# Layer 0's attention in two parts a batch with a written TensorE order, and its experts in groups of one and three batches

## The chip, the cores and the metric

The kernel runs on one core of one Trainium2 chip. The metric is device time in microseconds, from the first to the last instruction of an execution. The times of the kernel before are 1352.45 us (median of three runs, 1351.14 to 1359.07). A profiled execution is a run by itself and has its own time.

## What is computed

Four layers follow each other on x (4 batches of 512 tokens, 128 wide). Each layer adds a cross-attention with a context of 154 rows and then a mixture of eight experts; both read a layer norm of x without weights:

```python
x = x + _L0_xattn_ref(_layernorm(x), ctx_1024, ...)
x = x + _L0_ffn_ref(_layernorm(x), ...)
...
```

Layer 0's attention scores every token against the context rows, takes the softmax over the context and, with the maxima of the scores, one softmax over the tokens of a batch:

```python
A = jax.nn.softmax(Sim, axis=2)
hq_hat = jnp.einsum('bij,bjd->bid', A, decoder_hq)
Batt = jax.nn.softmax(jnp.max(Sim, axis=2), axis=1)
hc_bar = jnp.einsum('bi,bid->bd', Batt, encoder_hc)[:, None, :]
feats = jnp.concatenate([encoder_hc, hq_hat, encoder_hc * hq_hat, encoder_hc * hc_hat], axis=-1)
hcq = feats @ W_qv + b_qv
```

Layer 0's experts are gated (silu of one product times another, then a down projection), with the best two of eight for every token. Layers 1 to 3 have 16 heads of attention; layer 1 takes one expert a token with a capacity, layers 2 and 3 take two.

## The kernel before, in words

All data are float32. A tile is 128 tokens, so a batch has four tiles and the whole x has sixteen; x stays in SBUF, one buffer a batch.

The experts run on blocks of 128 tokens of one expert. route() finds for a group of batches (a "half": batches 0 and 1, or 2 and 3) the best experts, gives each token a slot in an array of blocks (at most 2 x 8 + 7 = 23 blocks a half in layer 0) and queues one row transfer for each tile and choice: an indirect DMA on POOL that scatters 128 rows of xn to buf in DRAM (line 722). experts() loads four blocks of tokens at a time (line 840, which waits for all scatters of the half), transposes them, and for every block loads the weights of its expert by a register (516 KB, line 869, three buffers), multiplies up (line 877), applies the activation (lines 900 and 905), multiplies down (line 916), copies the result (line 925) and stores it to ybuf (line 928). gather() queues indirect DMAs that bring the rows back (line 953), and combine() adds them to x with their weights (line 971).

Row transfers wait in the list rows_due. row_transfers(n, behind) starts the next n of them, and makes each wait for the instruction behind, so that they are spread over other work. They go behind copies: of attention (lines 1034, 1039, 1072, 1080), of a block's result (line 924) or of a narrow tile (line 375). A call without behind starts what is left.

Generators carry the interleaving. route() and experts() stop at each yield, and the class Steps advances them. In the main loop (from line 1356) the two halves of a layer follow each other: attention of all batches with the routing of half 0 beside it; experts of half 0, with the routing of half 1 advanced two steps for every two blocks; experts of half 1, with the gathers and sums of half 0 beside them; then the next layer's attention of batch 0, with the gathers and sums of half 1 beside it.

Layer 0's attention (layer0_setup, lines 974 to 1085) has prepare(), which gives a batch's normed x, its transpose and the scores, and tile_of(): scaled softmax, transposes (1033, 1038), the product with the context (1041, 1042), the maximum over the batch by a transpose and a broadcast matmul (1048 to 1052), the second softmax (1057), its sum over tokens (1060, 1061), the weights wc (1070), twelve matmuls with W_qv (1078) and the residual (1081, 1083). attend_first() (line 1278) calls these with nothing written about the order of engines: the framework's scheduler places the instructions on every engine. From layer 1 on attend_all() fixes the order of TensorE and ScalarE (layers 2 and 3 also that of VectorE) by the order in which the code is called.

In layer 1's attention (narrow_period, line 435) a tile's scores, maxima (294), exponentials (308), transposes (371) and products with the values (408) are laced with those of the tile before. The parts of the next batch (masks; norm and values; xnT; keys and queries) are handed out over the four tiles of a batch (line 1193).

Of the kernel before, what the change touches and what calls it, by code (L numbers as in the profile page):

```python
# [9 lines left out]
F32 = mybir.dt.float32  # L10
# [9 lines left out]
P = 128  # L20
# [9 lines left out]
NH = NT // 2  # L30
EPS = 1e-5
NEG = -1e20
BLK = (2 * NH + E - 1, NH + E - 1)
UPS = (2, 1, 1, 1)
NF = (4, 4, 2, 4)
PER = (1, 2, 2, 2)


# [9 lines left out]
def tile_xattn_moe_stack(ctx: ExitStack, tc: tile.TileContext, a: dict, out: bass.AP):  # L48
# [101 lines left out]
    for base, sign in ((0, 1), (D // H - 1, -1)):  # L150
# [17 lines left out]
    fill = const.tile([P, E, NH], F32, name="fill")  # L168
    nc.gpsimd.iota(
        fill, pattern=[[0, E], [P, NH]], base=0, channel_multiplier=0, allow_small_or_imprecise_dtypes=True  # L170
# [6 lines left out]
    nth = const.tile([1, BLK[0], E], F32, name="nth")  # L177
    nc.gpsimd.iota(
        nth, pattern=[[1, BLK[0]], [0, E]], base=0, channel_multiplier=0, allow_small_or_imprecise_dtypes=True
# [59 lines left out]
    def norm(src, found, pool=None):  # L239
        mv, rstd = found  # L240
        xn = (pool or xnp).tile([P, NI, D], F32, tag="xn", name="xn", bufs=3 if pool else 2)
        for i in range(NI):
            nc.vector.tensor_scalar(
                xn[:, i, :], src[:, i, :], mv[:, i, 0:1], rstd[:, i : i + 1], ALU.subtract, ALU.mult
            )
        return xn
# [23 lines left out]
    class Tile:  # L270
# [31 lines left out]
        def exp(self, g):  # L302
            if g == 0:
                self.pr = p2.tile([P, H, S2], F32, tag="probs", name="probs")
            for s in range(min(3, 8 - 3 * g)):
                for j in range(2):
                    h = self.at.heads(None, 3 * g + s, j)
                    nc.scalar.activation(  # L308
# [5 lines left out]
                    )  # L314

# [44 lines left out]
        def take_ends(self, engine):  # L360
            self.tails = p2.tile([self.rows, 4, P], F32, tag="tails", name="tails")
# [174 lines left out]
    def attention64(b, gather_x, wq, wk, wv, wo, add):  # L536
# [36 lines left out]
        def values_ends():  # L573
# [3 lines left out]
            for r in range(2):  # L577
                rows = slice(64 * r, 64 * r + 64)
                nc.tensor.matmul(q[rows, :], ct2[:, b], wv[:, r * 512 : (r + 1) * 512], start=True, stop=True)
# [6 lines left out]
            at.vt = at.vt.rearrange("p c s d -> p (c s d)")  # L586

# [35 lines left out]
    def rsm(name, *shape, dt=F32):  # L623
        return rt.tile([P, *shape], dt, tag=name, name=name)

    def top(lg):

        m = rt.tile([P, NH], F32, tag="m", name="m", bufs=4)
        nc.vector.tensor_reduce(m, lg, AX.X, ALU.max)
        eq = rt.tile([P, NH, E], F32, tag="eq", name="eq", bufs=4)  # L630
        nc.vector.tensor_tensor(eq, lg, bc(m, 2, E), ALU.is_equal)
        nc.vector.tensor_tensor(eq, eq, bc(rev_e, 1, NH), ALU.mult)
        r = rt.tile([P, NH], F32, tag="r", name="r", bufs=4)
        nc.vector.tensor_reduce(r, eq, AX.X, ALU.max)
        oh = rt.tile([P, NH, E], F32, tag="oh", name="oh", bufs=4)
# [5 lines left out]
    def row_transfers(n=2 * NH, behind=None):  # L641
# [9 lines left out]
    def route(layer, half, wg, bg, b2):  # L651

        lg = rsm("lg", NH, E)
        found = [stats(x[2 * half + k]) for k in range(B // 2)]
        yield
        xns = [norm(x[2 * half + k], found[k], rt) for k in range(B // 2)]
        yield  # L660
        xnTs = [transposed(xn) for xn in xns]
        yield
        for k, xnT in enumerate(xnTs):
            q = ps_tr()
            for i in range(NI):
                nc.tensor.matmul(q[:, i * E : (i + 1) * E], xnT[:, i * P : (i + 1) * P], wg, start=True, stop=True)
            o = lg[:, k * NI : (k + 1) * NI, :]
            qv = q[:, 0 : NI * E].rearrange("p (i e) -> p i e", i=NI)
            if bg is None:
                nc.vector.tensor_copy(o, qv)  # L670
            else:
                nc.vector.tensor_tensor(o, qv, bc(bg, 1, NI), ALU.add)
        yield
# [3 lines left out]
        sel = rsm("sel", NH + 1, E, dt=BF16)  # L677
        nc.vector.memset(sel[:, NH, :], 0.0)
        if layer == 1:
            nc.vector.tensor_copy(sel[:, 0:NH, :], oh1)  # L680
        else:
            yield
            lg2 = rsm("lg2", NH, E)
# [3 lines left out]
            nc.vector.tensor_tensor(sel[:, 0:NH, :], oh1, oh2, ALU.add)  # L687
# [3 lines left out]
        n = (NH + 1) * E  # L691
        q = ps_tr()
        nc.tensor.matmul(q[:, 0:n], before, sf, start=True, stop=False)
        for s in range(1, NH + 1):
            nc.tensor.matmul(q[:, s * E : n], ones_b, sf[:, 0 : n - s * E], start=False, stop=(s == NH))
        rk = rsm("rk", NH + 1, E)
# [736 lines left out]
```

## Time and profile before

| what | value |
|---|---|
| median of three runs | 1352.45 us |
| the profiled execution | 1282.47 us |
| its span | 1280.8 us |
| its mean granted TensorE clock | 0.917 |
| busy: TensorE, weight loads, VectorE, ScalarE, GpSimd | 1089.4, 896.9, 731.6, 565.3, 253.6 us |
| moved by DMA | 126.77 MB, mean 99 GB/s |

The profiled execution is 70 us shorter than the median of the runs. Stage by stage, from the chain of waits: layer 0's attention until about 106 us, its experts until about 259, layer 1's attention until about 479, its experts until about 560; layer 2 until about 891 and layer 3 to the end. In the profile's lines a start time and a duration in us come first; PE is TensorE, PEld its weight loads, DVE VectorE, ACT ScalarE, POOL GpSimd, SPq the queue of SyncE on which plain DMAs are issued. In a timeline the bracket at a line's end is the idle time before the instruction and what ended it. An x count of matmuls counts passes; a float32 matmul takes two where its form isn't a transpose.

### The profile page before, as it was taken

The page shows a single profiled execution, that of the slowest core. Times are in us where ns is not written, and L with a number is a line of the kernel's source. Part 1 is how long each engine was busy: PE and PEld are TensorE (multiplying, and loading weights), DVE is VectorE, ACT ScalarE, POOL GpSimd, SP SyncE. Part 2 cuts the span into 40 slices and gives each one's busy share as a digit, 9 for nine tenths or more (in the row PEclk, how much of TensorE's full clock was granted, in tenths as well). Part 3 has the DMA queues.
Part 4 walks back from the last instruction along what each step waited for, and adds up shares of the span by engine and source line. Part 5 has one row for each costly group of instructions (what it writes and reads, how often), then busy time and mean ns, then how long its engine had stood idle before and what let it go on. Part 6 is the DMA issues. An engine that isn't in the chain of part 4 may idle for free.

```text
span 1280.8 us, 26318 instructions
## 1 busy us (share of the span) xinstructions
PE 1089.4 (85%) x9351; PEld 896.9 (70%) x9351; DVE 731.6 (57%) x2012; ACT 565.3 (44%) x2264; POOL 253.6 (20%) x281
## 2 busy tenths in 40 slices
PE   4787998977878888889999998966899999899990
PEld 3657998933435448787878777855778788789890
DVE  6554646567666763335665776424476576646352
ACT  2113433454554543546656565321656665532230
POOL 2041315023000010232000004045220000402334
PEclk8767999988898988998999999887999999999996
DMA  7023786721100314433112214444421111334762
GB/s 228 1 81 113 216 253 189 207 94 25 23 19 26 100 38 119 133 110 84 35 35 55 64 37 123 123 150 133 127 55 45 41 35 35 109 95 143 209 191 60
DMA packets 136064, 126.77 MB, mean 99 GB/s; under 512 B 12538, under 2 KB 115583, under 8 KB 135551
## 3 DMA queue, kind: packets, MB, share of 16 engines
q1 hardware_dynamic: 128767, 110.39, 30.5%
q0 software_dynamic: 7168, 14.69, 3.9%
q8 instruction: 77, 1.26, 0.4%
q14 instruction: 52, 0.43, 0.1%
HBM read 101.31 MB, written 23.72 MB: 98 GB/s over the span
## 4 chain that ended last, share of the span: by engine, by line
PE 59%; DVE 12%; DMA 9%; issue 8%; ACT 5%; POOL 5%; SPq 2%; POOLq 0%; DVEq 0%
PE sc L877 11%; PE av L916 6%; PE tr L371 6%; PE sc L607 5%; PE av L408 5%; PE tr L425 5%; PE sc L592 3%; DMA yg<-ybuf,su 3%; POOL yg L953 3%; ACT probs L308 3%; DVE nm L294 3%; PE sc L1175 2%; DMA w<-in_up 2%; PE av L390 2%; PE tr L358 2%
## 5 line engine op out<-in xcount | busy, mean ns | idle before, releaser
L308 ACT ACTIVATE probs<-sc,nm 128x154 f32<-128x154 f32 x768 | 286.9, 403 | 162.7 <-DVE nm L294 162.5
L877 PE MATMUL sc<-tokT,w 128*128 128x128 f32 x1528 | 201.3, 286 | 8.7 <-DMA w<-in_up 3.6
L877 PEld LDWEIGHTS sc<-tokT,w 128*128 128x128 f32 x1528 | 189.0, 200 | 15.5 <-ACT eg L900 5.2
L294 DVE TENSOR_REDUCE nm<-sc 128x6 f32<-128x924 f32 x144 | 142.6, 1007 | 74.8 <-PE sc L607 49.1
L308 ACT ACTIVATION_READ_ACCUMULATOR probs<-sc,nm 128x1 f32 x768 | 168.3, 219 | 0.0
L916 PE MATMUL av<-w,hT 128*128 x1160 | 155.3, 279 | 3.2 <-DVE hT L905 2.5
L953 POOL DMA_INDIRECT yg<-ybuf,su x112 | 106.7, 952 | 246.5 <-ACT pT L267 59.9
L722 POOL DMA_INDIRECT buf<-xn,su x112 | 109.6, 979 | 227.0 <-DVE eb L745 97.3
L916 PEld LDWEIGHTS av<-w,hT 128*128 128x128 f32 x1160 | 141.9, 193 | 8.9 <-issue 4.7
L236 POOL TENSOR_TENSOR rstd<-ve,nhalf 128x4 f32<-128x4 f32 x32 | 33.0, 1032 | 547.3 <-DVE ve L234 429.6
L264 DVE COPY pT<-tr 128x512 f32<-128x512 f32 x160 | 106.9, 684 | 45.3 <-PE tr L371 41.5
L408 PE MATMUL av<-pT,vm 128*64 128x128 f32 (+1 forms) x1536 | 106.2, 284 | 22.5 <-DVE pT L264 22.4
L371 PE MATMUL tr<-ident,probs 128*128 128x128 f32 x768 | 123.1, 291 | 1.5 <-DVE rT L337 1.5
L371 PEld LDWEIGHTS tr<-ident,probs 128*128 128x128 f32 x768 | 86.1, 146 | 33.4 <-issue 21.7
L408 PEld LDWEIGHTS av<-pT,vm 128*64 128x64 f32 (+1 forms) x1536 | 63.8, 126 | 55.7 <-DVE pT L264 30.9
L900 ACT ACTIVATE eg<-sc,w 128x128 f32<-128x128 f32 x184 | 52.9, 368 | 89.5 <-PE sc L877 82.1
L607 PE MATMUL sc<-kT,qT 64*128 64x154 f32 x1024 | 87.1, 308 | 4.8 <-ACT probs L308 4.8
L905 DVE SCALAR_TENSOR_TENSOR hT<-sc,w,eg 128x128 f32<-128x128 f32 x184 | 56.2, 342 | 51.0 <-ACT eg L900 51.0
L607 PEld LDWEIGHTS sc<-kT,qT 64*128 64x128 f32 x1024 | 71.3, 189 | 15.8 <-issue 9.9
L592 PE MATMUL sc<-xnT,wq 128*128 128x128 f32 x512 | 73.6, 303 | 4.7 <-ACT probs L308 2.3
L592 PEld LDWEIGHTS sc<-xnT,wq 128*128 128x128 f32 x512 | 67.3, 212 | 10.2 <-issue 3.6
L425 PE MATMUL tr<-wo,aT 128*128 128x128 f32 x512 | 66.2, 284 | 1.6 <-DVE xnT L256 1.3
(255 smaller groups left out, 1432.2 us busy)
## 6 DMA issues: line engine op xcount, KB each, us to landing
w<-in_up SPq DMA_DIRECT2D x46, 516.0 KB
w<-in_up SPq DMA_DIRECT2D x76, 258.0 KB
rep<-rd SPq DMA_DIRECT2D x64, 256.0 KB
tok<-buf SPq DMA_DIRECT2D x36, 256.0 KB
ybuf<-ys SPq DMA_DIRECT2D x58, 128.0 KB
w<-in_down SPq DMA_DIRECT2D x3, 2048.0 KB
w<-in_up SPq DMA_DIRECT2D x46, 128.0 KB
ybuf<-ys SPq DMA_DIRECT2D x52, 64.0 KB
```

Of the source, the lines that this page charges most:

```text
L264: return nc.vector.tensor_copy(o, i)
L294: nc.vector.tensor_reduce(self.at.heads(self.nm, g, n), self.sc[g][:, :, 0 : n * S2].rearrange("p j (s k) -> p j s k", s=n), AX.X, ALU.max ...
L308: nc.scalar.activation(self.pr[:, h, :], self.sc[g][:, j, s * S2 : (s + 1) * S2], AF.Exp, bias=self.nm[:, h : h + 1], accum_out=self.rs[:, ...
L371: nc.tensor.transpose(q[:, t * P : (t + 1) * P], self.pr[:, h, 0:P], ident)
L408: nc.tensor.matmul(av[rows, cols], v, self.pT[n][:, t, :], start=False, stop=last)
L425: nc.tensor.matmul(o[:, 0:D], self.aT[:, c, :], self.at.wo[:, c, :], start=(c == 0), stop=(c == self.nb - 1))
L592: nc.tensor.matmul(sc[:, c // 4, c % 4 * P : (c % 4 + 1) * P], wq[:, c * P : (c + 1) * P], at.xnT[:, i * P : (i + 1) * P], start=True, sto ...
L607: nc.tensor.matmul(sc[:, j, s * S2 : (s + 1) * S2], at.qT[i][rows, c, :], at.kT[rows, c, :], start=True, stop=True)
L722: ins = nc.gpsimd.indirect_dma_start(out=buf[half], out_offset=bass.IndirectOffsetOnAxis(ap=su[:, t : t + 1], axis=0), in_=xns[t // NI][:, ...
L877: nc.tensor.matmul(dst, w[:, b, at : at + P], xT, start=True, stop=True)
L916: nc.tensor.matmul(y[:, b * D : (b + 1) * D], hT[:, fc, :], w2[:, bass.ds(es[b], 1), fc, :].rearrange("p o d -> p (o d)"), start=(fc == 0) ...
L953: ins = nc.gpsimd.indirect_dma_start(out=yg[:, t, :], out_offset=None, in_=ybuf[half], in_offset=bass.IndirectOffsetOnAxis(ap=su[:, t : t ...
```

## The change

Groups. In layer 0 the experts' groups are batch 0 alone (15 blocks at most, 8 scatters) and batches 1 to 3 (31 blocks, 24 scatters); the other layers keep two and two. The routing's tiles, lists and counts take the group's size; several small tiles of the routing get one buffer where they had two or four, and tails gets one where it had two. The gathered rows lie in tiles of one batch and one choice (six buffers of half the former size where there were two), and combine() starts gathers that haven't been started.

Order. attend_first() is written anew: it runs under a written order of TensorE alone, each batch's attention is cut in two by a yield ahead of the sum over tokens, and the steps of both groups' routings stand between these parts. In layer 0 the routing goes batch by batch without stops between statistics, norm and transposes. In the attention the transpose of the maximum and its reduction stand ahead of the product with the context.

Moves. Layer 1's setup (and its DMAs) is called behind the experts of group 0, not behind the attention. In layer 1's attention batch 1 is summed and its statistics taken at the second tile of batch 0, so the norm of the next batch moves one part later and xnT joins the keys and queries in the last. During the very first tile of layer 1 three row transfers are started behind the exponentials of each of its three groups of heads; there were none there. In the layer 0 attention, as before, two row transfers go behind a copy.

```diff
+GROUPS = (((0,), (1, 2, 3)), *(((0, 1), (2, 3)),) * 3)
+MOST = NI * max(len(g) for gs in GROUPS for g in gs)
...
+def most_blocks(layer, half):
+    return TOP[layer] * NI * len(GROUPS[layer][half]) + E - 1
...
     def exp(self, g):
...
+            if self.at.dh < 64 and self.at.first and self.i == 0:
+                row_transfers(3, ins)
...
-            self.tails = p2.tile([self.rows, 4, P], F32, tag="tails", name="tails")
+            self.tails = p2.tile([self.rows, 4, P], F32, tag="tails", name="tails", bufs=1)
...
     def route(layer, half, wg, bg, b2):
...
+        for some in ([b] for b in batches) if layer == 0 else (batches,):
+            found = [stats(x[b]) for b in some]
+            if layer:
+                yield
+            new = [norm(x[b], f, rt) for b, f in zip(some, found)]
+            if layer:
+                yield
+            xnTs = [transposed(xn) for xn in new]
+            if layer:
+                yield
+            for xnT in xnTs:
...
+            yield
...
+    class Gathered:
+        def __init__(self, choices):
+            self.rows = [p2.tile([P, NI, D], F32, tag="yg", name="yg", bufs=6) for _ in range(choices)]
+            self.begun = 0
...
+    def combine(layer, half, k, i, routed, got):
...
+        while got[k].begun < NI * len(routed[1]):
+            row_transfers(1)
...
         def tile_of(b, xn, xnT, sim, m, rs):
...
-            hq = ps_av()
-            nc.tensor.matmul(hq, cm[:, b, :], pm, start=True, stop=False)
-            nc.tensor.matmul(hq, ctail[:, b, :], pt, start=False, stop=True)
             m1 = small.tile([P, 1], F32, tag="m1", name="m1")
             nc.vector.tensor_reduce(m1, m, AX.X, ALU.max)
...
             nc.vector.tensor_reduce(m0, q[0:1, 0:P], AX.X, ALU.max)
+            hq = ps_av()
+            nc.tensor.matmul(hq, cm[:, b, :], pm, start=True, stop=False)
+            nc.tensor.matmul(hq, ctail[:, b, :], pt, start=False, stop=True)
             nc.tensor.matmul(q[:, P : P + 1], ones[0:1, :], m0, start=True, stop=True)
...
             nc.scalar.activation(ebt, md, AF.Exp, accum_out=es)
+            yield
             hcp = ps_av()
...
-            at.parts = ((masks,), (xn, values), (xnT,), (keys_queries,))
+            at.parts = ((masks,), (values,), (xn,), (xnT, keys_queries))
...
     def attend_first(layer, prepare, found):
-        tiles = [prepare(b, found[b]) for b in range(2)]
-        tiles[0](0)
-        tiles.append(prepare(2, found[2]))
-        tiles[1](0)
-        beside = Steps(route(layer, 0, *gates[layer])).step(3)
-        tiles.append(prepare(3, found[3]))
-        beside.step(5)
-        tiles[2](0)
-        beside.step(1)
-        tiles[3](0)
-        return beside.finish()
+        first, second = (Steps(route(layer, half, *gates[layer])) for half in range(2))
+        with tc.manual_schedule(engines={mybir.EngineType.PE}):
+            tiles = [prepare(b, found[b]) for b in range(2)]
+            tiles[0].step()
+            tiles[0].finish()
+            tiles.append(prepare(2, found[2]))
+            tiles[1].step()
+            first.step()
+            tiles[1].finish()
+            first.step(2)
+            tiles.append(prepare(3, found[3]))
+            first.step()
+            tiles[2].step()
+            first.step()
+            second.step()
+            tiles[2].finish()
+            first.step(2)
+            tiles[3].step()
+            tiles[3].finish()
+            first.finish()
+            second.step()
+        return first.result, second
...
+                        if GROUPS[layer - 1][1][0] == 1 and b == 0 and i == 1:
+                            found[1] = stats(x[1])
...
-        if layer < 3:
+        if 0 < layer < 3:
             prepare = setups[layer + 1]()
...
         got = gather(layer, 0, routed[0], stores)
         if layer < 3:
+            if layer == 0:
+                prepare = setups[1]()
             at = prepare(0, found)
```

## The prediction, made before the result was known

> **What bounds the kernel now.** I read the page first (span 1280.8 us, TensorE busy 85%), cut the span where the work changes hands (the table of stretches), and then read the chain of waits and the order of instructions of single engines around those cuts. The stretches below are layer 0's attention, layer 0's experts and layer 1's attention of batch 0; the columns are us, busy time of PE, weight loads, DVE, ACT and POOL, TensorE clock, DMA share and GB/s.
>
> ```profile
> 0.00:106.30 106.30, 69.16 (x318) 53.69 (x318) 61.49 (x252) 16.67 (x55) 29.25 (x49) 0.74 0.32 99
> 106.30:259.20 152.90, 146.56 (x1212) 141.13 (x1213) 84.38 (x321) 61.07 (x197) 32.82 (x34) 0.97 0.67 202
> 259.20:311.40 52.20, 37.13 (x239) 17.68 (x237) 36.15 (x91) 24.63 (x116) 17.43 (x18) 0.87 0.23 71
> ```
>
> The first stretch is a chain of dependences at a low clock, the second is TensorE without gaps (146.56 of 152.90), the third is a mix. What lies behind 311 us changes only in small ways, so the forecast is made here. The chain of waits shows how the first stretch ends:
>
> ```profile
> 85.05 4.26 PE av L1078 x20
> ...
> 98.54 0.70 DVE res L1081
> ...
> 99.52 1.34 POOL buf L722
> ...
> 101.17 2.25 DMA buf<-xn,su
> ...
> 103.57 2.73 DMA tok<-buf
> ...
> 106.34 1.99 PE tr L850 x8
> 108.33 5.88 PE sc L877 x32
> ...
> 115.98 1.79 PE sc L877 x16
> ```
>
> TensorE is done with attention at 98.5; the last pair of row transfers (scatters) is tied to the last residual, and from its end (99.2) to the first expert matmul at 108.2 pass 9.0 us. A matmul pass takes 4.26/20 = 0.213 us here and 1.79/16 = 0.112 us later: half clock and full clock. The timeline of TensorE has two more holes, both waits for the routing of batches 0 and 1:
>
> ```profile
> 57.49 1.42 PE L251 MATMUL tr<-ident,xn 128*128 128x128 f32 x8 [4.37 <-DVE xn L243]
> ```
> ```profile
> 68.67 0.24 PE L693 MATMUL tr<-sel,before 128*128 128x72 bf16 x1 [5.48 <-DVE sel L687]
> ```
>
> In the second stretch POOL issues the second half's scatters, one each 1.26 us (0.96 and 0.30 between), in pairs behind the blocks' result copies; they end at 164.4 while the first half's experts run on to about 178, so nobody waits:
>
> ```profile
> 140.15 1.03 POOL L722 DMA_INDIRECT buf<-xn,su  x1 [36.86 <-DVE eb L745]
> 141.49 0.96 POOL L722 DMA_INDIRECT buf<-xn,su  x1 [0.30 <-issue]
> ...
> 163.44 0.96 POOL L722 DMA_INDIRECT buf<-xn,su  x1 [0.30 <-issue]
> ```
>
> Layer 1 begins with a slow store (the 2 MB of weights are issued ahead of it), and its first gather comes at 274.11; DVE's in-order queue then meets gathers that have not landed:
>
> ```profile
> 261.66 0.34 SPq L822
> 262.10 7.12 DMA ybuf<-ys
> ...
> 274.11 1.01 POOL yg L953
> ```
> ```profile
> 277.16 0.35 DVE L971 SCALAR_TENSOR_TENSOR x<-yg,wa,x 128x128 f32<-128x128 f32 x1 [1.58 <-DMA yg<-ybuf,su]
> ```
>
> [...]
>
> **The change part by part** (us of the profiled execution).
>
> 1. *Attention of layer 0.* Group 0 is batch 0 alone: 8 scatters, not 16. Its routing waits for batch 0's residual (40.6 before), not batch 1's (54.6), but in the new order its vector steps are laced into tiles 1 and 2, so the slots come about when they came (72.5), no earlier than 66. 8 x 1.27 = 10.2 ends them near 83, under tiles 2 and 3. So the 9.0 us tail leaves the path. In its place TensorE's written order runs, behind the last tile, the bias matmuls of batch 0 (8 passes of L801, 1.4), batch 2's transposes and router matmuls with a copy between (0.9 + 0.6 + 1.0), and the first token transposes with their copy (1.0 + 0.7): 5.6. Gain: 108.2 - 98.5 - 5.6 = 4.1. The two holes (4.37 + 5.48 = 9.85) are waits for a routing that the tiles no longer stand behind; a written order has holes of its own (tile b+1 follows tile b, where two tiles interleaved), so I take 8. Moving the maximum's transpose ahead of the hq matmuls is inside these 8. Together -12. Ends: -4 if the holes only move, -25 if TensorE gets its full clock: from 20 to 100 us it is busy 14.46, 12.60, 13.37 and 19.41 at 0.66, 0.78, 0.67 and 0.61, which at 1.0 would be 40.2 in place of 59.8; some two thirds of that 19.6 lie on the chain (13).
>
> 2. *The boundary between the two groups.* All of layer 0 still has 46 blocks (15 + 31 for 23 + 23). But now 24 scatters, not 16, have to get under 15 blocks, not 23. The slots of group 1 are emitted after 6 blocks (before: 8); each later block copy releases two: the copies of blocks 5 to 14 make 20, and 4 are left with no copy to go under. POOL keeps pace (2 x 1.27 = 2.5 against 2.9 to 3.3 us a block) but not more. Behind the last copy: start 0.3, five more at 1.27 (6.35), then from the last one's start to the first expert matmul as at 101.17 to 108.24 (7.07): 13.7, plus the copy itself 0.35, less 0.9 of token transposes that are due anyway: +13.1. TensorE has nothing else in its queue there but two small value matmuls (0.8). After it the clock is cold: 5.88 - 3.6 = +2.3. Weight loads queued on SP behind the token load lose nothing, three blocks' weights stand ready. Together +15.5; from 11 (warm clock, faster landing) to 18 (POOL a pair behind).
>
> 3. *Group 0's gathers*, 8 in place of 16, under group 1's experts. Before, DVE stood behind the first ones and TensorE lost 2.5 us at 198 and then a cold block (3.34 - 1.79 = 1.55). Now DVE's order has one more block ahead of the first sum. Taken -3; 0 to -4.
>
> 4. *Layer 1, batch 0.* 24 gathers in place of 16, and batch 1's statistics. Nine are released by the exponentials of the first tile, so they start when the slow store lands (262.10 + 7.12 = 269.2, five earlier than 274.11). 24 x 1.26 = 30.2 and two rstd of 1.04 put the last landing near 269.4 + 32.3 + 1.7 = 303.4; before it was 302.6. But in DVE's queue the last sum now stands ahead of tile 1's aT, which ran at 299.36: +4. From 0 (the later periods absorb it) to +10 (each early stall shifts maxima and pT copies by itself).
>
> 5. *Parts of layer 1.* xnT and its consumer now share the last tile of a batch: TensorE waits for the 0.68 us copy, three times: +2.3, 0 to 3. Single buffers for tails, eq and the like are written once a period and read before the next; the work between hides them at 0, a few tenths a tile if not. Later setup of layer 1 lies under the experts: 0; uncovered some 2.
>
> Sum: -12 + 15.5 - 3 + 4 + 2.3 = +6.8, a span of 1287.6. The runs' median, 1352.45, is 70 over the profiled run's 1282.47; terms 2 and 4 are POOL and DMA time, which a slower TensorE doesn't stretch, so I add the sum as it is: 1359.
>
> **Rivals.**
> A, the forecast: an earlier start paid back at the boundary, 1359; own range 1346 to 1367; chance 0.48.
> B, the written order keeps TensorE warm: term 1 becomes -25, sum -6, 1346. For: in 80 to 100 it is busy 19.4 of 20. Against: the clock there was 0.61 all the same. 0.18.
> C, the boundary is hidden: if group 1's slots come some four blocks earlier (12 us), POOL's 30 us fit and term 2 falls to about +1: sum -8, 1345, or 1332 with B's clock. Against: the routing's vector steps stand in DVE's queue between the blocks' products. 0.12.
> D, slower: DVE's queue behind gathers. Its first sums stand ahead of tile 1's maxima and pT copies; if each of some eight stops costs 1.2 us that ACT and TensorE can't take back, term 4 is +12 and, with the slower end of term 1 (-9), the sum is 12 + 15.5 - 9 - 3 + 2.3 = +18: 1370. It decides from about +10 in term 4 on. For: waits of 1.58 and more at 277. 0.20.
> The change not doing what it says: the order is written out and the group sizes fix the counts, so only 0.02.
>
> **How the numbers follow.** About 1% (13.5 us: under 1339, over 1366) is what a measurement can tell. Faster: half of B, half of C, the rest: 0.09 + 0.06 + 0.02 = 0.17. Slower: nearly all of D and A's top, 0.19 + 0.04 = 0.23. Within: 0.60. The range 1336 to 1373 leaves about one tenth on each side.
>
> **What would show it.** Right: first L877-type matmul near 96; a TensorE idle of 12 to 15 us at about 145 to 160 that ends with the token load, with six scatters back to back in it; no hole at 198; layer 1's batch 0 taking some 56 us. Wrong: the matmuls start after 103 or before 88; no hole between the groups; a stretch behind 320 that differs by more than 3 us.

## The result and the profile after

Twenty runs of each kernel, on one chip: 1358.13 us after (1352.34 to 1364.00) against 1353.8 us before (1342.29 to 1360.08), a ratio of 1.004 with a 95% interval of 1.0021 to 1.0058. The forecast was 1359 and "within 1%". Whether its terms were right too is what the experiments ask: several of them were off, in both directions.

One fact has to come first. The chips of this study differ. The kernel before took a median of 1277.6 and 1278.5 us in two series of runs and 1345.3, 1348.6 and 1353.8 us in three others; below these are called the quick and the slow chips. (Each chip that the record names was used at one time only, so whether the chip or the hour makes the difference is not shown.) The first profile of before (span 1280.8) agrees with a quick chip, the profile of the result (span 1355.7) is from a slow one. Laid side by side, these two profiles differ by 75 us, of which the change has about 4. So stretches are compared between profiles of quick chips, and a ratio always with the runs of before on the same chip.

The stretches of the kernel after, first on the slow chip of the result, are cut where the first expert matmul starts, at the copy of block 16's result (the first of group 1), at the last result copy of layer 0, and at the fourth and the sixteenth residual of layer 1. The columns are those of the prediction; its own cut for layer 1's first batch, 311.40, lies earlier than the fourth residual.

```profile
0.00:90.20 90.20, 65.86 (x314) 51.84 (x314) 56.90 (x241) 17.59 (x56) 21.10 (x41) 0.79 0.40 116
90.20:170.40 80.20, 65.24 (x498) 61.84 (x499) 37.36 (x142) 24.78 (x76) 23.33 (x25) 0.87 0.52 157
170.40:259.10 88.70, 86.63 (x735) 82.68 (x733) 48.22 (x174) 36.77 (x122) 8.68 (x9) 1.00 0.67 206
259.10:346.50 87.40, 57.41 (x361) 27.60 (x361) 52.62 (x133) 36.96 (x181) 26.43 (x27) 0.77 0.17 53
346.50:512.00 165.50, 138.56 (x1158) 80.65 (x1158) 107.95 (x239) 83.50 (x386) 10.98 (x11) 0.94 0.19 52
```

The first expert matmul (L899, L877 before) starts at 90.22; before it was 108.24. The chain of waits shows what stands ahead of it now: no row transfer, only TensorE's own order with two copies in between.

```profile
81.01 4.48 PE av L1115 x24
85.49 1.08 PE av L823 x8
86.57 0.60 PE tr L260 x4
...
87.25 0.59 ACT xnT L102
...
87.89 1.06 PE tr L687 x8
88.95 0.50 PE tr L872 x4
...
89.47 0.70 DVE tokT L98
```

(x24 are the last batch's twelve products with W_qv, two passes each; in the first profile of before the 48 products of L1078 count x96, the 128 transposes of L251 x128.) From the end of the attention's matmuls (85.49) to the experts (90.22) pass 4.7 us, the 5.6 of the prediction less a little. From the same point 9.7 passed before (98.5 to 108.24); the prediction's 9.0 is counted from the end of the last residual. The bill comes at the boundary between the groups, in the same chain:

```profile
152.21 0.28 DVE ys L947
...
152.77 0.96 POOL buf L744
...
154.03 0.89 POOL buf L744
...
155.29 0.96 POOL buf L744
...
156.56 2.25 DMA buf<-xn,su
...
158.96 2.70 DMA tok<-buf
...
161.70 1.97 PE tr L872 x8
```

The last four transfers are released by the copies of the last two blocks (152.21 and 154.57); then come the landing, the token load and eight transposes. TensorE's timeline gives the wait: its group 0 ends at 153.96 and the next instruction stands 7.74 us:

```profile
161.70 1.97 PE L872 MATMUL tr<-ident,tok 128*128 128x128 f32 x8 [7.74 <-DMA tok<-buf]
```

The third place is the first tile of layer 1. Four names are needed here: rT holds the transposed reciprocals of the softmax sums, tails and pT the transposed exponentials, and aT the product with the values. In VectorE's timeline three sums with gathered rows stand between the first and the second maxima of the second tile, ahead of the first tile's rT, and the first two wait for the gathers. The transpose that rT copies was done at 266.96 in TensorE's timeline, and the copy ran at 273.68, behind these sums. TensorE's row shows who pays; the second row is the same transpose in the first profile of before:

```profile
265.37 1.06 DVE L303 TENSOR_REDUCE nm<-sc 128x6 f32<-128x924 f32 x1
269.79 0.41 DVE L1007 SCALAR_TENSOR_TENSOR x<-yg,wa,x 128x128 f32<-128x128 f32 x1 [3.36 <-DMA yg<-ybuf,su]
271.32 0.35 DVE L1007 SCALAR_TENSOR_TENSOR x<-yg,wb,x 128x128 f32<-128x128 f32 x1 [1.12 <-DMA yg<-ybuf,su]
...
272.33 0.40 DVE L1007 SCALAR_TENSOR_TENSOR x<-yg,wa,x 128x128 f32<-128x128 f32 x1
272.65 1.11 DVE L303 TENSOR_REDUCE nm<-sc 128x6 f32<-128x924 f32 x1
273.68 0.27 DVE L348 COPY rT<-tr 16x128 f32<-16x128 f32 x1
```
```profile
274.00 1.12 PE L382 MATMUL tr<-ident,probs 128*128 128x128 f32 x4 [6.61 <-DVE rT L348]
```
```profile
272.44 0.66 PE L371 MATMUL tr<-ident,probs 128*128 128x128 f32 x4 [0.76 <-DVE rT L337]
```

### The profile page after: what moved, and what is told of

It reads as the page before. It is cut to its first block, busy times and chain, and to the rows that moved or that the text cites. A ratio compares the mean times of both kernels' runs of the same rounds, so it can differ in the third digit from the quotient of the medians.

```text
span 1355.7 us, 26297 instructions
## 1 busy us (share of the span) xinstructions
PE 1114.9 (82%) x9351; PEld 914.6 (67%) x9351; DVE 730.2 (54%) x2012; ACT 565.0 (42%) x2264; POOL 254.0 (19%) x281
## 3 DMA queue, kind: packets, MB, share of 16 engines
q8 instruction: 77, 1.26, 0.4%
## 4 chain that ended last, share of the span: by engine, by line
PE 62%; DVE 14%; issue 8%; DMA 6%; ACT 4%; POOL 2%; another core or an unknown queue 2%; SPq 2%; POOLq 0%; DVEq 0%; ACTq 0%
PE sc L899 12%; PE av L938 9%; PE tr L382 6%; PE av L419 5%; PE sc L619 5%; PE tr L436 5%; PE sc L604 3%; DVE nm L303 3%; ACT probs L317 2%; PE sc L1213 2%; PE av L401 2%; POOL yg L983 2%; PE tr L369 2%; DVE pT L273 2%
## 5 line engine op out<-in xcount | busy, mean ns | idle before, releaser
L899 PE MATMUL sc<-tokT,w 128*128 128x128 f32 x1528 | 206.1, 289 | 9.8 <-issue 3.3
L899 PEld LDWEIGHTS sc<-tokT,w 128*128 128x128 f32 x1528 | 193.9, 204 | 15.7 <-issue 6.0
L938 PE MATMUL av<-w,hT 128*128 x1160 | 162.5, 284 | 36.7 <-issue 21.2
L938 PEld LDWEIGHTS av<-w,hT 128*128 128x128 f32 x1160 | 145.9, 197 | 45.0 <-issue 25.8
L744 POOL DMA_INDIRECT buf<-xn,su x112 | 109.3, 976 | 226.2 <-DVE ve L243 54.5
L245 POOL TENSOR_TENSOR rstd<-ve,nhalf 128x4 f32<-128x4 f32 x32 | 33.1, 1035 | 578.4 <-DVE ve L243 516.1
L419 PE MATMUL av<-pT,vm 128*64 128x128 f32 (+1 forms) x1536 | 108.4, 286 | 28.6 <-DVE pT L273 26.8
L382 PEld LDWEIGHTS tr<-ident,probs 128*128 128x128 f32 x768 | 87.4, 147 | 39.8 <-issue 23.3
L419 PEld LDWEIGHTS av<-pT,vm 128*64 128x64 f32 (+1 forms) x1536 | 63.8, 127 | 64.3 <-DVE pT L273 37.6
L947 DVE COPY ys<-av 128x256 f32<-128x256 f32 (+1 forms) x110 | 38.8, 356 | 102.1 <-PE av L938 63.3
L619 PEld LDWEIGHTS sc<-kT,qT 64*128 64x128 f32 x1024 | 71.4, 189 | 15.7 <-issue 9.9
L436 PE MATMUL tr<-wo,aT 128*128 128x128 f32 x512 | 72.7, 302 | 2.4 <-DVE xnT L265 1.3
```

The source lines that it names most:

```text
L382: nc.tensor.transpose(q[:, t * P : (t + 1) * P], self.pr[:, h, 0:P], ident)
L419: nc.tensor.matmul(av[rows, cols], v, self.pT[n][:, t, :], start=False, stop=last)
L436: nc.tensor.matmul(o[:, 0:D], self.aT[:, c, :], self.at.wo[:, c, :], start=(c == 0), stop=(c == self.nb - 1))
L619: nc.tensor.matmul(sc[:, j, s * S2 : (s + 1) * S2], at.qT[i][rows, c, :], at.kT[rows, c, :], start=True, stop=True)
L744: ins = nc.gpsimd.indirect_dma_start(out=buf[half], out_offset=bass.IndirectOffsetOnAxis(ap=su[:, t : t + 1], axis=0), in_=xns[t // NI][:, ...
L899: nc.tensor.matmul(dst, w[:, b, at : at + P], xT, start=True, stop=True)
```

## The experiments

The theory: the change starts the experts some 18 us earlier and pays at two places, at the boundary (POOL's 24 transfers) and in layer 1's first batch (VectorE's queue behind gathers). The main rival: the boundary alone, or POOL's 24 gathers as such, with VectorE's order of no account; and that the loss belongs to the slow chip. Totals in microseconds that were expected early on were meant for a slow chip; where a run came from a quick one, its ratio is what can be compared.

**before_again: the kernel before, unchanged.**

> The kernel before, unchanged, for a second profile. Its first profiled execution took 1282.5 us where its 20 runs take 1342 to 1360. If that profile was only an unusually short execution, this one has a span of 1340 to 1358, with the same first 260 us to within 3 us and the other 60 to 75 us spread over layers 1 to 3 as engines that wait for nothing the profile shows. If the profile was typical in its stretches and the other runs lose time outside of them, the span is again near 1281 and the stretches of layers 1 to 3 agree with the first profile to 3 us. Against itself the ratio is 1.000.

Median 1277.13 on a chip where the other runs of before have 1277.56: neither a short execution nor time lost outside the stretches; what fits is another chip. Its stretches, cut at the same places:

```profile
0.00:111.00 111.00, 72.61 (x327) 55.65 (x327) 61.91 (x253) 16.70 (x55) 28.82 (x49) 0.70 0.31 95
111.00:167.10 56.10, 55.90 (x475) 54.71 (x475) 30.98 (x125) 25.52 (x77) 15.24 (x16) 0.96 0.67 196
167.10:264.20 97.10, 90.10 (x746) 85.71 (x746) 54.32 (x200) 36.96 (x122) 17.50 (x19) 0.98 0.68 204
264.20:336.70 72.50, 51.78 (x362) 23.99 (x361) 47.53 (x113) 37.00 (x181) 17.36 (x18) 0.89 0.19 57
336.70:503.10 166.40, 141.71 (x1158) 83.71 (x1158) 108.08 (x239) 83.33 (x386) 10.96 (x11) 0.91 0.19 52
```

They agree with the first profile of before (108.2, 56.1, 97.3, 72.3, 166.2) to 0.2 us, but for the start, which varies by 2.8 from execution to execution.

**after_again: the kernel after, unchanged.**

> The kernel after, unchanged, for a profile beside the others of this study: its first profile comes from a chip on which both kernels take some 1355 us, the first one of before from one where before takes 1278. Theory 1: the same change shows on either chip. On a chip at 1278: first expert matmul at 89 to 91, last result copy of layer 0 (261.7 and 264.2 in the two profiles of before) at 253 to 257, from there to the first residual of layer 1 35 to 37 us (26.6 before), ratio 1.002 to 1.006. Theory 2: the loss behind layer 0 belongs to the slow chip alone, and here the start's gain stays: ratio 0.990 to 0.996.

On another quick chip: ratio 0.9999 (0.9981 to 1.0016), median 1277.65. So it is no loss there and a small one on the slow chip, but no gain on either. Theory 2 falls, and theory 1 holds in part: the first residual comes 35.7 us after the last result copy, as it had it, but that copy is at 251.61, earlier than its 253 to 257, and the ratio is below its 1.002 to 1.006. The stretches, to be read against the five lines above:

```profile
0.00:91.20 91.20, 64.55 (x315) 50.81 (x315) 57.11 (x241) 17.57 (x56) 21.18 (x41) 0.81 0.38 115
91.20:163.00 71.80, 61.63 (x498) 59.21 (x499) 37.08 (x142) 24.77 (x76) 23.17 (x25) 0.89 0.59 175
163.00:251.60 88.60, 85.72 (x734) 82.49 (x734) 47.91 (x173) 36.63 (x121) 8.69 (x9) 1.00 0.67 207
251.60:333.70 82.10, 55.21 (x364) 26.23 (x363) 52.50 (x134) 37.20 (x181) 26.14 (x27) 0.81 0.19 57
333.70:495.40 161.70, 135.06 (x1158) 78.75 (x1157) 107.78 (x238) 83.47 (x386) 10.98 (x11) 0.96 0.20 53
```

Start -19.8 (-17.0 against the first profile), group 0 with the boundary +15.7, the rest of the experts -8.5, layer 1's first batch +9.6, its other batches -4.7.

**order_alone: the written order with groups of two and two.**

```diff
-GROUPS = (((0,), (1, 2, 3)), *(((0, 1), (2, 3)),) * 3)
+GROUPS = (((0, 1), (2, 3)),) * 4
...
```

(The lines left out move two steps of the routing between the parts of the attention.)

> The kernel after with the old groups of two and two batches in layer 0, its attention still in two parts a batch in a written order of TensorE, layer 1's parts as after. Theory 1 (the start gains, the boundary between the groups takes it back): 16 scatters again, 8 of them under the last tile and 8 behind it (8 x 1.27 = 10 us), so the first expert matmul at 97 to 101 (90.2 after, 108.2 before), no hole of TensorE between the groups, total 1347 to 1353. Theory 2 (what was given back comes from layer 1's attention, not the boundary): 1360 or more, since the start gains less and layer 1 costs the same.

Ratio 1.0006 (0.9982 to 1.0030), median 1279.73. The first expert matmul comes at 105.92, later than expected, and the hole between the groups is gone: the copy of block 16 stands 1.2 us ahead of its place in the first profile of before, as block 15's does (1.0). The boundary cost therefore belongs to the groups of one and three. But the total was missed by theory 1, since the first residual of layer 1 still comes 34.8 us after the last result copy (26.6 before), with 16 gathers, and TensorE waits 8.80 us for rT. The loss in layer 1 needs no 24 gathers.

**groups_alone: the groups without a written order.**

```diff
-        with tc.manual_schedule(engines={mybir.EngineType.PE}):
...
+        tiles[0].finish()
+        tiles.append(prepare(2, found[2]))
+        tiles[1].finish()
+        first.step()
+        tiles.append(prepare(3, found[3]))
+        first.step(4)
+        tiles[2].finish()
+        first.step()
+        tiles[3].finish()
+        first.finish()
+        second.step(2)
```

> The kernel after with layer 0's attention in the scheduler's own order, one tile after another in the source as before and no written order; groups batch 0 and batches 1 to 3 kept, routing of batches 1 and 2 still ahead of the experts. Theory 1 (the written order is worth about half of the start, the small group the other half): first expert matmul at 97 to 102, the hole at the boundary unchanged at 12 to 14 us more than before, total 1365 to 1370. Theory 2 (the small group alone makes the start): first expert matmul at 89 to 93, total 1356 to 1360.

Ratio 1.0032 (1.0007 to 1.0058), median 1280.57, with the experts starting at 86.39, earlier even than theory 2's 89. The start is made by the small group; theory 1's halves fall. TensorE even keeps its wait for the routing, the one that the written order was to remove, and loses nothing at the end by it:

```profile
62.47 0.22 PE L715 MATMUL tr<-sel,before 128*128 128x40 bf16 x1 [5.04 <-DVE sel L709]
...
86.39 1.86 PE L899 MATMUL sc<-tokT,w 128*128 128x128 f32 x7 [0.79 <-DVE tokT L98]
```

One execution is not enough to say that the scheduler's order is better: the same attention starts the experts at 91.86 in combo_late below, and the four quick profiles with the written order and the small group lie between 88.90 and 91.62. The ratio, a little above after_again's, comes from another chip and the intervals overlap, so it doesn't show what the written order is worth in the total. But it is not what raises the clock: over the start the clock is 0.84 here and 0.78 in combo_late without it, 0.74 in order_alone with it, and 0.74 and 0.70 in the two profiles of before.

**relief: four row transfers behind a copy in group 0.**

```diff
-                2 * n, nc.vector.tensor_copy(ys[:, 0:n], y[:, 0 : n * D].rearrange("p (b d) -> p b d", b=n))
+                (4 if layer == 0 and half == 0 else 2) * n, nc.vector.tensor_copy(ys[:, 0:n], y[:, 0 : n * D].rearrange("p (b d) -> p b d", b=n))
```

> The kernel after, but in layer 0's first group each copy of a block's result releases four row transfers in place of two, so that all of group 1's are released within four blocks of the slots. Theory 1 (the boundary is a matter of when the scatters are released): POOL runs them one behind the other, 24 x 1.27 = 30.5 us from 114, the last at 143 to 146 and so before the last block of group 0; the hole of 13 us goes and the total is 1344 to 1349. Theory 2 (packed scatters slow the weight loads beside them, or POOL cannot start earlier): blocks 6 to 15 get longer by as much, total 1355 to 1362.

Ratio 1.0005 (0.9985 to 1.0025). POOL runs the last sixteen one behind the other, as its timeline shows, but the last starts 32.8 us after the first, where in after_again it is 33.1:

```profile
114.02 1.04 POOL L744 DMA_INDIRECT buf<-xn,su  x1 [24.04 <-DVE sl L737]
...
122.94 0.96 POOL L744 DMA_INDIRECT buf<-xn,su  x1 [0.30 <-issue]
127.89 0.96 POOL L744 DMA_INDIRECT buf<-xn,su  x1 [3.99 <-DVE ys L947]
129.16 0.97 POOL L744 DMA_INDIRECT buf<-xn,su  x1 [0.30 <-issue]
...
146.83 0.95 POOL L744 DMA_INDIRECT buf<-xn,su  x1 [0.30 <-issue]
```

So on a quick chip the boundary is POOL's pace from the slots on (24 x 1.26 = 30.2 us and one gap), not the number released behind a copy. TensorE still waits for the token load, 10.49 us (8.44 in after_again). The second half of theory 2 holds. On the slow chip of the result it is otherwise: there the same 24 transfers run from 114.08 to 156.56, 42.5 us in place of 33.1, because POOL stands between them (8.70 us ahead of the ninth, 2.46 ahead of the last four) until the next block's copy releases more. Whether four a copy would help on such a chip was not tried.

**late_gathers: without the transfers behind layer 1's first exponentials.**

```diff
-            if self.at.dh < 64 and self.at.first and self.i == 0:
-                row_transfers(3, ins)
```

> The kernel after without the row transfers that layer 1's first exponentials release, so that its gathers are released where the sums ask for them or behind copies, as before. In DVE's order the first sum then stands behind the first tile's rT, tails and first pT copies, where in the kernel after three sums stand ahead of the second tile's maxima and of rT. Theory 1 (DVE's queue behind gathers is what layer 1's first batch loses): from the last result copy of layer 0 to the first residual 27 to 29 us (35 to 37 after), total 3 to 8 us below the kernel after, ratio to before 0.996 to 1.001. Theory 2 (24 gathers on POOL set the end of the batch whatever DVE's order): the first tile is quick, but tiles 2 to 4 wait for gathers that start later, total 0 to 5 us above the kernel after.

Ratio 0.9928 (0.9902 to 0.9954), median 1267.49: more than theory 1 asked for. In VectorE's timeline the maxima, rT, tails and two pT copies now run through, and the first sum comes behind them:

```profile
258.28 1.12 DVE L303 TENSOR_REDUCE nm<-sc 128x6 f32<-128x924 f32 x1 [0.36 <-PE sc L1211]
259.31 0.27 DVE L346 COPY rT<-tr 16x128 f32<-16x128 f32 x1
...
261.29 0.69 DVE L273 COPY pT<-tr 128x512 f32<-128x512 f32 x1 [0.26 <-PE tr L380]
...
264.59 0.35 DVE L1005 SCALAR_TENSOR_TENSOR x<-yg,wa,x 128x128 f32<-128x128 f32 x1 [1.81 <-DMA yg<-ybuf,su]
```

The first residual comes 24.9 us after the last copy (35.7 in after_again) and the first batch takes 71.0 us in place of 82.1, with the same 24 gathers, the last of which even starts later (304.94 against 298.89). Theory 2 falls.

**store_first: layer 1's down weights behind the last store.**

```diff
...
-        w2 = load_down(layer)
+        w2 = load_down(layer, stores if layer == 1 else ())
```

(load_down makes its DMA wait for the last of the stores that it is given.)

> The kernel after with layer 1's 2 MB of down weights loaded behind the last store of layer 0's results in place of ahead of it. Theory 1 (the gathers start late because that store shares the DMA engines with the 2 MB): the first gather comes 4 to 6 us earlier, 2.5 to 4 us after the last result copy (8.4 in the profiles so far), DVE waits less at its first sums, total 2 to 5 us below the kernel after. Theory 2 (what counts is the place of the sums in DVE's order; the schedule now puts five sums ahead of the second tile's maxima where three stood): no gain or up to 5 us lost.

Ratio 1.0007 (0.9977 to 1.0036). The first gather comes at 255.70, 2.7 us after the last result copy (8.5 in after_again), as theory 1 had it, and nothing is won, as theory 2 had it. Here seven sums stand ahead of the second tile's second maxima, which start at 266.45, and so ahead of rT, and the first residual comes after 34.3 us. Earlier gathers drew their sums forward with them.

**combo_late: the groups without a written order, with relief, store_first and late_gathers.**

> Groups of batch 0 and batches 1 to 3, layer 0's attention in the scheduler's own order, four row transfers behind a copy in layer 0's first group, layer 1's down weights behind the last store, and no transfers behind layer 1's first exponentials: every part that the runs so far speak for. Theory 1 (gains of layer 0 are kept if layer 1's DVE queue is mended): last result copy of layer 0 at 244 to 250 where the chip takes 1278 for before, first residual 26 to 29 us later, ratio to before 0.989 to 0.994. Theory 2 (24 gathers set layer 1's first batch): ratio 0.997 to 1.003.

Ratio 0.9898 (0.9869 to 0.9927), median 1263.68, the lowest of the study, as theory 1 had it, though its interval overlaps that of late_gathers. The last result copy is at 251.99, later than expected, the first residual 24.6 us behind it.

**sums_late: early gathers, late sums.**

```diff
...
-            nc.vector.scalar_tensor_tensor(xi, yg[:, i, :], cw[:, t : t + 1], xi, ALU.mult, ALU.add)
+            ins = nc.vector.scalar_tensor_tensor(xi, yg[:, i, :], cw[:, t : t + 1], xi, ALU.mult, ALU.add)
+            if layer == 0 and half == 1:
+                wait_for(ins, gate, "behind the first copy of the tile before")
```

(gate holds the first pT copy of the period.)

> The kernel after with all its transfers behind layer 1's first exponentials kept, but each sum of group 1 made to wait for the first pT copy of the period in which it is written, so that in DVE's order the first sum stands behind the first tile's rT, tails and pT copies as it does in late_gathers, while the gathers still start early. Theory 1 (the place of the sums in DVE's order costs it, not the early gathers): first residual of layer 1 25 to 28 us after layer 0's last result copy (35.7 in after_again, 24.9 in late_gathers), ratio to before 0.990 to 0.994, no worse than late_gathers. Theory 2 (the early gathers themselves disturb the first tile, by their DMA traffic or on POOL): the first residual stays at 32 us or more, ratio 0.997 to 1.001.

On a slow chip: 1.0060 (1.0037 to 1.0082), first residual after 34.6 us. By the first residual theory 2; the ratio lies outside both ranges, which were set for a quick chip. But the timelines of VectorE and TensorE show that the edit only moved the sums one copy further. Six of them stand one behind the other ahead of the second pT copy, wait 5.10 us for their gathers, and TensorE waits 5.14 for that copy:

```profile
271.06 0.27 DVE L348 COPY rT<-tr 16x128 f32<-16x128 f32 x1
...
274.30 0.35 DVE L1011 SCALAR_TENSOR_TENSOR x<-yg,wa,x 128x128 f32<-128x128 f32 x1 [1.15 <-DMA yg<-ybuf,su]
276.87 0.35 DVE L1011 SCALAR_TENSOR_TENSOR x<-yg,wa,x 128x128 f32<-128x128 f32 x1 [2.21 <-DMA yg<-ybuf,su]
278.96 0.36 DVE L1011 SCALAR_TENSOR_TENSOR x<-yg,wa,x 128x128 f32<-128x128 f32 x1 [1.74 <-DMA yg<-ybuf,su]
...
279.77 0.68 DVE L273 COPY pT<-tr 128x512 f32<-128x512 f32 x1
```
```profile
280.50 0.66 PE L422 MATMUL av<-pT,vm 128*32 128x128 f32 x8 [5.14 <-DVE pT L273]
```

By its total the run therefore doesn't separate the early gathers from the place of their sums. The first tile does. Its gathers start as early as in the result (8.4 us after the last result copy), yet rT comes 10.6 us after that copy and the first pT copy 11.6, exactly as in early_slots and late_again below, the two slow-chip runs with the same groups and without early transfers; in the result rT came after 14.9. The second pT copy, which stands behind the waiting sums, comes after 19.3 us, where these two have it at 12.5. So the early gathers by themselves don't hold up the first tile; sums placed ahead of it do.

**early_slots: late_gathers with the second routing laced into fewer blocks.**

```diff
-            first.step(2 // PER[layer])
+            first.step(1 if layer == 0 else 2 // PER[layer])
```

> late_gathers, with one block of layer 0's first group in place of two between two steps of the second group's routing, so that the slots of batches 1 to 3 are written after some 4 blocks and not 6. Theory 1 (the hole between the groups is POOL's 24 transfers from the slots on, 24 x 1.27 = 30.5 us plus a release gap of 3 to 5): slots 4 to 7 us earlier, TensorE's wait for the token load shrinks from 8 to 9 us to 2 to 5, total 3 to 6 us below late_gathers, ratio to before 0.987 to 0.991. Theory 2 (the routing's vector steps hold up the blocks' products by as much as the slots come earlier): blocks 3 to 6 longer by 4 to 6 us, total within 2 us of late_gathers (0.991 to 0.995).

On the slow chip of sums_late: 0.9978 (0.9958 to 0.9999). The first transfer of group 1 starts at 115.32, no earlier than in sums_late (113.06): the routing's vector steps now stand between the products of blocks 4 and 5, and block 5's copy comes 10.2 us later than there (119.5 against 109.3). TensorE's wait for the token load stays at 7.78 us. Theory 2 in its mechanism; the ratio lies outside both ranges, which were set for a quick chip. The ratio of late_gathers on a slow chip, below, is no worse.

**order_late: order_alone without the transfers behind the exponentials.**

> order_alone (groups of two and two, written order of TensorE) without the transfers behind layer 1's first exponentials. If the groups of one and three are what is worth having once layer 1 is mended, this one is 4 to 8 us above late_gathers, ratio to before 0.996 to 1.000, since layer 0 ends only some 5 us earlier than before. If the early transfers were all that the change lost and the groups bring nothing net, it is level with late_gathers at 0.991 to 0.995.

On the same slow chip: 1.0040 (1.0017 to 1.0062), with the experts starting at 109.51. Its first residual comes 25.2 us after the last copy (34.8 in order_alone), so the layer 1 loss is gone here too; the total misses the expected 0.996 to 1.000, and where it lies cannot be said, as before has no profile from a slow chip.

**late_again: late_gathers on another chip.**

> late_gathers once more, for another chip: so far it was timed on one where before takes 1278, and early_slots and order_late on one where before takes 1345. Theory 1 (the early transfers cost layer 1's first batch some 10 us on any chip): where before takes 1340 or more, the ratio is 0.994 to 0.998 (1.004 for the kernel after on such a chip, less 10 us) and the first residual of layer 1 comes 25 to 27 us after layer 0's last result copy; where before takes 1278, 0.990 to 0.996 again. Theory 2 (the gain belongs to the quick chip): ratio 1.000 or more where before takes 1340 or more.

On a slow chip: 0.9958 (0.9937 to 0.9979), median 1342.86. Theory 1. In its profile (a long execution, span 1353.9) layer 1's first batch takes 76.5 us against the 87.4 of the result's, and its first residual comes after 26.3 (39.4 there); early_slots, a shorter execution on a slow chip, has 75.1 and 26.2. On slow chips, three series of runs, the ratios now stand so: with early transfers 1.004, without them 0.9958, without them and with groups of two and two 1.004. By these the groups of one and three are worth some 0.8% (11 us) there once layer 1 is mended. The only pair on one chip, early_slots and order_late, differs by 8.9 us, with the slots moved as well. Their profiles differ by 14.1 us, of which 8.2 lie in layer 1's later batches (163.9 against 172.1), whose code hardly differs, so how much the groups are worth by themselves is not shown.

## Why the prediction was right, and where it wasn't

The number and the forecast of no clear change were right, the sum less so: +6.8 was forecast, the runs have +4.3 (a ratio of 1.004) on the slow chip and -0.8 (0.9999) on a quick one. By its steps:

1. *Attention, -12 forecast.* Mis-sized: -17.0 to -19.8 on quick chips, inside the ends of -4 and -25. The tail's part was right (9.7 us replaced by 4.7 to 5.2). The rest was laid to the written order and its two holes. The holes did close (the rows at 57.49 and 68.67 have no successor in after_again), but groups_alone kept one of 5.04 us and began no later. Nor does the written order bring much by itself: order_alone starts the experts 2.3 to 5.1 us earlier than before, and order_late, on a slow chip, at 109.51. What made the start is the group of one, with 8 transfers and a routing that needs one batch. The clock helped: 0.81 against 0.74 and 0.70 over the stretch, TensorE busy 64.6 us in place of 71.0 and 72.6. That is some of rival B's gain, but not its cause: the clock rose in groups_alone without the written order (0.84) and not in order_alone with it (0.74). That keeping TensorE busy would raise its clock was the author's estimate in B, and the profiles don't show it: in the first profile of before it was busy 19.4 us of 80 to 100 at a clock of 0.61, in after_again 16.5 us of 60 to 80 at 0.91.
2. *Boundary, +15.5 forecast.* Right in size: the stretch from the first expert matmul to block 16's copy grew by 15.7 us, 13.6 of it between the copies of blocks 15 and 16 (16.3 us in place of 2.7) and 2.1 in the blocks ahead. The picture was partly wrong: TensorE's own wait is 7.7 to 8.4 us and not 12 to 15, and two or three transfers follow the last copy, not six. The rest lies in the transposes and in the slow matmuls behind the wait (32 passes in 4.7 to 4.9 us; in the profile of the result 4.91, at a granted clock of 0.77, where from 170.36 on 16 passes took 1.79). The prediction's +2.3 sets its 32 passes at 108.33 (clock 0.63) against 32 at 0.112 us, 3.6 in all; its half and full clock were granted clocks of 0.55 over the row at 85.05 and 1.00 over the row at 115.98. In the blocks ahead TensorE also waits 0.68 and 1.02 us for weights in after_again; behind the boundary they stood ready, as the prediction had it. On quick chips POOL's pace sets the end, as relief shows, so "POOL keeps pace" was too kind. Rival C failed: more release didn't hide it, and early_slots couldn't bring the slots earlier.
3. *Group 0's gathers, -3 forecast.* Too small: -8.5 for the rest of the experts. In before_again VectorE waits at most of its 16 sums (4.80 us at the first), and from block 25's copy to block 35's pass 38.5 us, against 28.6 in after_again: TensorE paid by slower blocks all through, not only in the one hole that was counted. With 16 gathers order_alone has 38.7 us there, too.
4. *Layer 1's first batch, +4 forecast.* The term that was mis-sized most: +9.6. The forecast looked at the last sum, ahead of a late aT. The loss is at the first sums, ahead of the second tile's maxima, rT and pT: the first residual is 9.1 us late at once. That is rival D's mechanism at nearly its price (+12, deciding from +10). late_gathers shows that the early transfers cost it: without them the first batch takes 71.0 us, less than before. That it is the queue and not the early gathers themselves is read from the waits of VectorE and TensorE and from the first tile of sums_late.
5. *Parts, +2.3 forecast.* Not seen: batches 1 to 3 take 161.7 to 167.1 us in the quick chips' profiles with the new parts, 166.2 and 166.4 before.

The steps were right in sign but for the last, but that the total came out was luck: a start and gathers that gained 10 to 13 us more than forecast were set off by a first batch of layer 1 that lost 5.6 more and by the slow chip's own losses. "A stretch behind 320 that differs by more than 3 us" did occur (-4.7), so one of the prediction's own signs of error was there. And adding the sum unchanged to a median 70 us above the profiled execution was a leap over a chip. POOL and the DMAs did keep their times on the slow one (1.26 us from one transfer to the next, 2.25 for the landing, 2.70 for the token load; 1.26, 2.25 and 2.73 in the first profile of before), but there group 0 with its boundary took 80.2 us where the quick one took 71.8, layer 1's first batch 87.4 in place of 82.1. From block 1's copy to block 16's pass 73.2 us there against 63.8; order_late has no such loss in the same blocks (50.9 us, 50.1 in order_alone on a quick chip). Part of it can be read from TensorE's timeline of the result: from 122.0 to 125.6 five waits name no releaser, 2.2 us in all, and the next 13 expert passes took 2.93 us; another part is POOL's wait for copies. That blocks with the routing of three batches suffer more on slow chips is what the profiles show; why, they don't.

## What to carry to other kernels

An early start is worth what the next engine's queue lets through (rT's copy ran 6.7 us after its transpose was done, behind the waiting sums, in the profile of the result): ask of each transfer released earlier which instructions the schedule then draws forward with it, and what stands behind them. A sum placed ahead of its data cost more here than the data's delay: starting gathers earlier drew sums forward with them and cost 10 us (after_again against late_gathers, on one chip). Where a unit keeps one pace per transfer, as POOL did here (1.26 us on the quick chips and on the slow one of the result), count transfers from the moment they can start to the moment they are needed; releasing more at a time changed nothing on the quick chip where it was tried. And compare two profiles only once both are known to come from like chips.

## What the runs showed of the hardware

The same kernel took 5 to 6% longer on some chips. For the kernel after, the mean clock was 0.902 against 0.923 and the span 78.9 us longer; TensorE was busy for 34.3 us of that (1114.87 against 1080.61) and idle for the rest. Part of the idle time has no releaser in the profile: ahead of the down matmuls of all layers TensorE stood 36.7 us on the slow chip, 21.2 of them so, and 1.4 on the quick one.

```profile
L938 PE MATMUL av<-w,hT 128*128 x1160 | 162.5, 284 | 36.7 <-issue 21.2 <-DVE st L236 10.9 <-DVE hT L927 2.8
```
```profile
L938 PE MATMUL av<-w,hT 128*128 x1160 | 155.0, 279 | 1.4 <-DVE mv L238 0.6 <-DVE hT L927 0.5
```

A 64 KB store issued just behind a 2 MB load took 7.14 us in the chain of waits of the result and 7.20 in that of after_again; with the load held back behind it, a store took 1.52 us in that of combo_late. In store_first the first gather came 5.8 us sooner after the last copy than in after_again.
